# First unit's second-layer weight sums on VectorE, and bias vectors' products held to their units

## Chip, cores and metric

The kernel runs on one core of a Trainium2 chip. The metric is the device time of one launch in microseconds (us), taken as the median over several runs.

## What is computed

The reference applies two layers to a batch of 2 images with 512 channels and 32 x 32 positions. Layer 0 is deformable attention with a learned position bias, then an output projection and an MLP. Layer 1 is plain attention over all 1024 positions. The part that the change touches is the end of layer 0 and the preparation of layer 1:

```python
# layer 0
out = jnp.einsum('bchw,oc->bohw', out, out_w) + out_b[None, :, None, None]     # output projection
x = x + out
xn2 = _bn(x, bn2_g, bn2_b)
h1 = jax.nn.gelu(jnp.einsum('bchw,oc->bohw', xn2, mlp_w1) + mlp_b1[...], approximate=False)
x = x + jnp.einsum('bchw,oc->bohw', h1, mlp_w2) + mlp_b2[...]
# layer 1
q = xt @ Wq.T + bq ; k = xt @ Wk.T + bk ; v = xt @ Wv.T + bv
attn = softmax(q @ k.T / sqrt(c)) ; out = (attn @ v) @ Wp.T + bp ; x = x + out
```

## The kernel before

**Tiling.** Channels lie on the 128 partitions, four blocks of channels per image. A matrix product of 512 x 512 weights with 512 x 1024 activations is done by a fast scheme with seven block products in place of eight (names 1 to 7 in `PARTS`, which gives the left and the right block of each). Each block product is eight multiplications of 128 x 128 by 128 x 512 on TensorE into one PSUM buffer of 128 x 1024. The scheme needs sums of the weights' blocks and differences of the activations' blocks. `fold` (L102) makes the four sums of a weight tile, on the engine that it is given (its instructions carry L105); `spread` (L107) makes the four differences of an activation tile on VectorE (L111 and L114). `plus` (L122) is the eviction of a PSUM buffer by an addition on VectorE (L123). `multiply` (L116) goes through the products in a given order and calls the eviction of each.

**Stages.** Most of the span, to about 1895 us, is the position bias: a long loop of small multiplications (L635). Then come, in order:

- `project(0)` and `project(1)` (L894): the output projection of the two images, with tiles `op0x`, `op0w`, `opt` and `op1x`, `op1w`. The evictions that also add the output bias are L908. PSUM is used through a pool of three buffers here, and a second small pool beside it.
- `normalise(0)` (L938): eight activations on ScalarE that make `xb`, the normalised first image; `spread` makes its differences.
- The MLP in eight units, (image, part) with four parts of 512 hidden channels each. A unit is `layer1` (L959: seven products into `hm`, GELU on ScalarE, `spread` of `hm`) and `layer2` (L992: seven products onto the residual `xs` or an accumulator `acc`). PSUM is used through a new pool of four buffers, `mq`, that takes the place of the earlier two. `normalise(1)` stands in the fourth unit.
- Layer 1 in the same manner (L1079 on).

**Weights of the MLP.** `load_unit` (L877) loads the two weight tiles of a unit, `w1t` and `w2t` (two buffers each, shared with `op1x` and `op1w`), from SP's queue, and makes the sums of both on GpSimd. The first unit's tiles are loaded amid the loads of `xs`; the second unit's when the projection has let go of the buffers; each later unit's when the unit two before it is done with its own.

**Bias vectors' products.** Layer 1's matrix for queries and keys is folded into one, and the value and output matrices into another. What is left of the bias vectors is eight products of a row block `wr` (128 x 512, loaded from `wlt`) with a broadcast row `br` (loaded from `brow`), summed along the row into one column of `ub`. One of them stands in each unit (L1060). `wr` has one buffer, so a load waits for the product before it; `br` changes after the fourth. GpSimd then makes `uc` (L1070) and adds `bp` (L1071). Their readers are in layer 1, from 2342 us on.

**Order.** The program text isn't the order of execution on an engine. A planner takes the traced instructions and orders each engine's queue by when, in its own reckoning, operands and buffers come free. `tc.issue_after(ins)` holds the instructions traced inside it behind `ins`, if they are on the same engine; it makes no wait between engines. `newest(engine)` (L253) gives the instruction traced last for an engine. Before, neither the sums nor the products of L1060 have such an edge.

## Time and profile before

| what | us |
|---|---|
| median of 3 runs (2647.37 to 2648.81) | 2648.25 |
| the profiled execution, its own time | 2648.76 |
| its span, first to last instruction | 2647.0 |
| TensorE busy (99% of the span) | 2628.8 |
| VectorE busy (85%) | 2240.1 |
| ScalarE busy (64%) | 1693.2 |
| GpSimd busy (30%) | 791.0 |

Times in the timeline count from the first instruction of the span. A row of the timeline has the start, the length, the engine, the line, the operation with the tiles that it writes and reads, the size and the number of instructions merged; in brackets stands the idle time of the engine before it, and what ended it. A row of the table by stretches has each engine's busy time with the count of instructions in brackets, and then the granted clock of TensorE.

### The profile page before, as it was taken

The page shows a single profiled execution, that of the slowest core. Times are in us where ns is not written, and L with a number is a line of the kernel's source. Part 1 is how long each engine was busy: PE and PEld are TensorE (multiplying, and loading weights), DVE is VectorE, ACT ScalarE, POOL GpSimd, SP SyncE. Part 2 cuts the span into 40 slices and gives each one's busy share as a digit, 9 for nine tenths or more (in the row PEclk, how much of TensorE's full clock was granted, in tenths as well). Part 3 has the DMA queues.
Part 4 walks back from the last instruction along what each step waited for, and adds up shares of the span by engine and source line. Part 5 has one row for each costly group of instructions (what it writes and reads, how often), then busy time and mean ns, then how long its engine had stood idle before and what let it go on. Part 6 is the DMA issues. An engine that isn't in the chain of part 4 may idle for free.

```text
span 2647.0 us, 46958 instructions
## 1 busy us (share of the span) xinstructions
PE 2628.8 (99%) x19368; PEld 953.9 (36%) x19368; DVE 2240.1 (85%) x1329; ACT 1693.2 (64%) x2222; POOL 791.0 (30%) x867
## 2 busy tenths in 40 slices
PE   9999999999999999999999999999999999999999
PEld 3333322333333233233333323333334444446454
DVE  7999999999999999999999999999674483466354
ACT  5887898888888878887887777777521131114041
POOL 1333333333333333333333333333432232000000
PEclk9999999999999999999999999999999999999999
DMA  5788977888878888887887888788721111000000
GB/s 188 178 178 173 199 166 167 179 182 197 177 169 180 178 178 193 173 177 169 182 183 169 176 177 182 168 174 185 193 96 33 47 48 48 0 17 0 32 1 32
DMA packets 116294, 366.77 MB, mean 139 GB/s; under 512 B 23376, under 2 KB 27616, under 8 KB 113392
## 3 DMA queue, kind: packets, MB, share of 16 engines
q0 software_dynamic: 69408, 235.31, 47.3%
q1 hardware_dynamic: 46240, 128.15, 13.7%
q8 instruction: 153, 2.51, 0.4%
q14 instruction: 61, 0.50, 0.1%
q10 hardware_dynamic: 432, 0.31, 0.0%
HBM read 74.81 MB, written 6.55 MB: 31 GB/s over the span
## 4 chain that ended last, share of the span: by engine, by line
PE 92%; DVE 3%; issue 2%; ACT 2%; DMA 1%; DVEq 0%; POOL 0%; SPq 0%; ACTq 0%; POOLq 0%
PE ps L635 62%; PE sw L953 15%; PE sw L1084 9%; PE sw L1182 2%; PE sim L721 1%; PE psg L537 1%; DVE h L618 1%; PE sw L900 1%; DVE ub L654 0%; DMA wr<-in_wlt 0%; PE pkv L471 0%; DVE xs L908 0%; PE sim L704 0%; PE pt L738 0%; DMA uc<-uo 0%
## 5 line engine op out<-in xcount | busy, mean ns | idle before, releaser
L635 PE MATMUL ps<-h,cw 128*32 128x512 f32 x16384 | 1776.4, 592 | 5.2 <-ACT rx L644 4.0
L618 DVE CUSTOM_DVE_ANT_1 h<-ta,tb 128x4096 f32<-128x4096 f32 (+1 forms) x257 | 1131.2, 4402 | 28.6 <-PE ps L635 25.8
L635 PEld LDWEIGHTS ps<-h,cw 128*32 128x32 f32 x16384 | 543.0, 110 | 1203.1 <-issue 1131.4
L644 ACT ACTIVATE rx<-ps,sc 128x1024 f32<-128x1024 f32 x512 | 567.9, 1109 | 145.1 <-PE ps L635 127.1
L646 ACT ACTIVATE ub<-ps,sc 128x1024 f32<-128x1024 f32 x256 | 308.2, 1204 | 93.6 <-PE ps L635 93.5
L654 DVE SCALAR_TENSOR_TENSOR ub<-rx,sc,ub 128x1024 f32<-128x1024 f32 x256 | 327.1, 1278 | 6.6 <-ACT ub L646 6.6
L673 POOL DMA_DIRECT2D ua<-uc x126 | 158.8, 1275 | 298.6 <-DMA ua<-uc 288.7
L673 POOL DMA_DIRECT2D ua<-ua x189 | 225.9, 1372 | 16.8 <-DMA ua<-uo 11.9
L953 PE MATMUL sw<-xb,w1t 128*128 128x512 f32 x448 | 195.2, 596 | 3.1 <-DVE xs L123 3.1
L656 POOL DMA_DIRECT2D uo<-ub x127 | 125.6, 989 | 233.0 <-DVE ub L654 217.8
L953 PE MATMUL sw<-hm,w2t 128*128 128x512 f32 x448 | 193.6, 592 | 0.0
L646 ACT ACTIVATE uo<-ps,sc 128x1024 f32<-128x1024 f32 x128 | 154.2, 1204 | 53.0 <-PE ps L635 52.7
L654 DVE SCALAR_TENSOR_TENSOR uo<-rx,sc,uo 128x1024 f32<-128x1024 f32 x128 | 163.7, 1279 | 9.0 <-ACT uo L646 9.0
L123 DVE TENSOR_TENSOR hm<-hm,sw 128x1024 f32<-128x1024 f32 x56 | 67.5, 1218 | 105.5 <-PE sw L953 105.3
L673 POOL DMA_DIRECT2D uc<-uo x63 | 53.6, 852 | 313.5 <-DMA uc<-uo 307.4
L953 PEld LDWEIGHTS sw<-xb,w1t 128*128 128x128 f32 x448 | 85.7, 192 | 111.5 <-issue 105.7
L962 ACT ACTIVATE hm<-hm,vs 128x512 f32<-128x512 f32 x64 | 42.5, 713 | 129.0 <-DVE hm L123 129.0
L953 PEld LDWEIGHTS sw<-hm,w2t 128*128 128x128 f32 x448 | 85.1, 190 | 107.1 <-issue 106.4
L123 DVE TENSOR_TENSOR xs<-xs,sw 128x1024 f32<-128x1024 f32 (+1 forms) x48 | 55.6, 1171 | 73.7 <-PE sw L1084 36.0
L656 POOL DMA_DIRECT2D ua<-ub x64 | 58.6, 915 | 179.1 <-DVE ub L654 171.8
L1084 PE MATMUL sw<-aT,vt 128*128 128x512 f32 x224 | 96.7, 593 | 0.3 <-ACT aT L1164 0.3
L987 ACT COPY hm<-sw 128x1024 f32<-128x1024 f32 x8 | 8.1, 1010 | 136.3 <-PE sw L953 136.3
(247 smaller groups left out, 2268.2 us busy)
## 6 DMA issues: line engine op xcount, KB each, us to landing
uo<-ub POOLq DMA_DIRECT2D x127, 512.0 KB, 5.5
fb<-fdr SPq DMA_DIRECT2D x64, 512.0 KB, 5.1
ua<-ub POOLq DMA_DIRECT2D x64, 512.0 KB, 5.5
uc<-ub POOLq DMA_DIRECT2D x64, 512.0 KB, 5.1
ua<-ua POOLq DMA_DIRECT2D x63, 256.0 KB, 6.2
ua<-uo SPq DMA_DIRECT2D x63, 256.0 KB, 2.6
ua<-uo POOLq DMA_DIRECT2D x63, 256.0 KB, 5.7
uc<-uc POOLq DMA_DIRECT2D x63, 256.0 KB, 6.7
```

Source lines behind the costliest of these rows:

```text
L123: nc.vector.tensor_tensor(out, a, b_, op)
L618: nc.vector._custom_dve(TENSOR_ADD_SAT, out=h1[:, y : y + step].rearrange("p y t x -> p (y t x)"), in0=a.unsqueeze(1).to_broadcast([P, ste ...
L635: nc.tensor.matmul(ps[32 * q : 32 * q + 32, h, :], cw2[:, 32 * z : 32 * z + 32], h1[:, 16 * h : 16 * h + 16, q, :], start=True, stop=True,)
L644: nc.scalar.activation(o, ps, AF.Relu, bias=sc[:, 4 + z : 5 + z])
L646: nc.scalar.activation(o, ps, AF.Relu, bias=sc[:, 4 + z : 5 + z], scale=sc[:, z : z + 1])
L654: nc.vector.scalar_tensor_tensor(r[1], r[0], sc[:, z : z + 1], r[1], ALU.mult, ALU.add)
L656: nc.gpsimd.dma_start(out=sums[s][1], in_=sums[s][3], accum_op=ALU.add)
L673: nc.gpsimd.dma_start(out=out, in_=in_, accum_op=ALU.add)
L953: nc.tensor.matmul(ps[:, m, :], w[:, a, k, m * P : (m + 1) * P], x[:, b_, k, :], start=(k == 0), stop=(k == 1),)
L962: nc.scalar.activation(hm[:, blk, m, :], src[:, m, :], AF.Gelu, bias=col("mb1", 4 * p + 2 * (blk // 2) + m), scale=scale,)
L1084: nc.tensor.matmul(ps[:, m, :], w[:, a, k, c + m * P : c + (m + 1) * P], x[b_][:, k, :], start=(k == 0), stop=(k == nk - 1),)
L1182: nc.tensor.matmul(v[:, m, :], xbl[b_][:, k, m * P : (m + 1) * P], gn[:, a, k, :], start=(k == 0), stop=(k == 1),)
```

## The change

Two things are changed. The four sums of the first unit's `w2t` are no longer made by GpSimd in `load_unit`; VectorE makes them, traced after `project(1)` and held behind the instruction that was traced last for VectorE, which is the last eviction of `project(1)`. And each of the eight products of L1060 is held behind the instruction traced last for VectorE at that point, which is the last difference of `hm` in its own unit's `layer1`. The helper `newest` is moved up so that both places can use it.

```diff
@@ -50,6 +50,9 @@
+    def newest(engine):
+        return next(i for i in reversed(nc.cur_bb.bb.instructions) if i.engine == engine)
@@ -249,9 +252,6 @@
-        def newest(engine):
-            return next(i for i in reversed(nc.cur_bb.bb.instructions) if i.engine == engine)
@@ -879,7 +879,8 @@
             for i, w in enumerate((w1, w2)):
                 wt = wp.tile([P, 7, 2, 256], F32, name=f"w{i + 1}t")
                 nc.sync.dma_start(out=wt[:, 0:4], in_=w[:, p])
-                fold(nc.gpsimd, [wt[:, j] for j in range(7)])
+                if (b, p, i) != (0, 0, 1):
+                    fold(nc.gpsimd, [wt[:, j] for j in range(7)])
                 ws_.append(wt)
@@ -1035,6 +1036,8 @@
         xb = normalise(0)
         spread(op1[1])
         project(1, *op1, op1w[:, 3:5].rearrange("p a k n -> p a (k n)"))
+        with tc.issue_after(newest(mybir.EngineType.DVE)):
+            fold(nc.vector, [wts[units[0]][1][:, j] for j in range(7)])
         spread([xb[:, j] for j in range(7)])
         load_unit(*units[1])
@@ -1057,9 +1060,11 @@
             layer1(p, wa, xb, hm)
-            nc.vector.scalar_tensor_tensor(
-                wr, wr, 1.0, br, ALU.mult, ALU.mult, accum_out=ub[:, j, k : k + 1]
-            )
+
+            with tc.issue_after(newest(mybir.EngineType.DVE)):
+                nc.vector.scalar_tensor_tensor(
+                    wr, wr, 1.0, br, ALU.mult, ALU.mult, accum_out=ub[:, j, k : k + 1]
+                )
             if p == NU - 1 and b == 0:
                 xb = normalise(1)
```

## Prediction

> **What bounds the kernel now.** I read the page first, then the busy time by stretches around the change, then the timeline of each engine there, and last the chain of waits. The page says that TensorE is busy for nearly the whole span:

> ```profile
> PE 2628.8 (99%) x19368; PEld 953.9 (36%) x19368; DVE 2240.1 (85%) x1329; ACT 1693.2 (64%) x2222; POOL 791.0 (30%) x867
> ```

> So only 18 us are not TensorE's. The table by stretches shows where part of them lie: one stretch has 21.29 of 26.90 us busy, and the next runs at a granted clock of 0.94.

> ```profile
> core 0: us, PE busy (x) PEld busy (x) DVE busy (x) ACT busy (x) POOL busy (x), PEclk, DMA share, GB/s
> 1911.50:1925.50 14.00, 14.00 (x36) 6.10 (x34) 13.96 (x11) 1.01 (x1) 12.64 (x7) 1.00 0.44 164
> 1925.50:1952.40 26.90, 21.29 (x50) 9.04 (x49) 24.11 (x32) 6.65 (x9) 0.64 (x1) 0.99 0.23 79
> 1952.40:1978.00 25.60, 25.60 (x56) 11.31 (x57) 11.44 (x12) 6.30 (x8) 15.86 (x13) 0.94 0.34 123
> ```

> The stretch is the output projection of the second image, project(1). TensorE's timeline names the releaser of each gap; all are VectorE's evictions of PSUM buffers:

> ```profile
> 1922.01 3.60 PE L900 MATMUL sw<-qa,vp 128*128 128x512 f32 x8
> 1927.28 3.70 PE L900 MATMUL sw<-qa,vp 128*128 128x512 f32 x8 [1.67 <-DVE xs L123]
> 1935.22 3.67 PE L900 MATMUL sw<-op1x,op1w 128*128 128x512 f32 x8 [0.81 <-DVE xs L908]
> 1952.32 25.85 PE L953 MATMUL sw<-xb,w1t 128*128 128x512 f32 x56 [3.12 <-DVE xs L123]
> 1978.00 24.20 PE L953 MATMUL sw<-hm,w2t 128*128 128x512 f32 x56
> ```

> VectorE's timeline shows what keeps it late. Between the evictions stand bias vectors' products (L1060), two of which wait for their row to arrive; and two operations take 2.28 us that take 1.22 elsewhere:

> ```profile
> 1914.67 2.28 DVE L114 SCALAR_TENSOR_TENSOR op1x<-op1x,qa 128x1024 f32<-128x1024 f32 x1
> 1916.88 2.28 DVE L111 TENSOR_TENSOR qa<-qa 128x1024 f32<-128x1024 f32 x1
> ...
> 1930.59 0.69 DVE L1060 SCALAR_TENSOR_TENSOR wr<-wr,br 128x512 f32<-128x512 f32 x1 [1.63 <-DMA wr<-in_wlt]
> ...
> 1950.43 0.69 DVE L1060 SCALAR_TENSOR_TENSOR wr<-wr,br 128x512 f32<-128x512 f32 x1 [0.77 <-DMA wr<-in_wlt]
> ...
> 1951.05 1.22 DVE L123 TENSOR_TENSOR xs<-xs,sw 128x1024 f32<-128x1024 f32 x1
> 1961.11 1.22 DVE L123 TENSOR_TENSOR hm<-hm,sw 128x1024 f32<-128x1024 f32 x1 [8.85 <-PE sw L953]
> ```

> GpSimd's sums lie beside the slow ones:

> ```profile
> 1909.90 5.97 POOL L105 TENSOR_TENSOR w1t<-w1t 128x512 f32<-128x512 f32 x4 [6.33 <-DMA w1t<-in_w]
> 1915.83 8.38 POOL L105 TENSOR_TENSOR w2t<-w2t 128x512 f32<-128x512 f32 x4
> ```

> The chain of waits agrees: from 1911 to 1952 it runs through VectorE and the loads of wr; after 1952.32 it is TensorE's multiplications alone.

> [...] 2.28 against 1.22 us beside the sums, while evictions, which read PSUM, keep 1.21 us at 1919.08. [...] Here a gap of 3.12 us sufficed: weight loads from 1952.3 to 1955.0 stand about 0.85 us apart instead of 0.43; after the gaps of 1.67 and 0.81 us none do.

> **The accounting.** A product is eight multiplications; seven take 24.03 us where nothing waits (2026.07 to 2050.10), so 3.433 each. From project(1)'s first product (1922.01) to the second unit's start (2002.04) are 80.03 us for 21 products, which need 72.10. The excess is 7.93: 1.84 and 0.98 at the two gaps, 0.18 at two restarts, 3.29 before layer1 of the first unit, and 1.65 in that layer1 (25.68 for 24.03), the slow restart. This is all that the change can win here.

> **The change part by part.**

> *GpSimd gives up four sums (8.38 us).* VectorE's L114 at 1914.67 is still blocked until the w1 sums end (1915.83), so it ends at 1916.95 as now. From there nothing blocks it: the difference qa ends at 1918.1, the eviction into opt at 1919.2, the next difference at 1920.35, the four L908 (2.73 for four uncontended, from 1945.80) at 1923.0 instead of 1926.1. That wins 3.1 us on VectorE. The two last evictions of project(0) end at 1924.15 and 1925.3; the first frees the buffer for the second product, which TensorE reaches at 1925.44. The gap of 1.67 goes.

> *Bias products leave project(1).* Five stand there, 0.70 us each with the accumulator read (3.5), and 2.4 us of waits on wr. What is late next is ScalarE: its eight normalising activations (5.75 us) wait for L908's last reading of opt, so they run 1923.1 to 1928.85; the difference L114 of xb needs the last, ends at 1930.2, and the two L908 behind it free product one's buffer at 1931.5. TensorE needs it at 1932.3: 0.8 us to spare, and the gap of 0.81 goes. With VectorE's order otherwise as now, its later evictions follow TensorE. The last product ends at 1946.04 (1922.01 + 7 x 3.433). Its eviction begins 0.20 later (as at 2012.54 for a product ended at 2012.34), takes 1.22, and TensorE starts 0.05 after that: 1.47 us, short enough not to halve the clock.

> *Four sums on VectorE.* One of this size takes 0.686 us there (op0w at 1431.4), 1.26 on GpSimd; four are 2.74. The edge puts them behind the last eviction, where VectorE now idles 8.85 us. Contended with GpSimd's sums for the second unit, which start about then, three of 1.26 us go between: 6.5 us, still inside. They are needed only in layer2, 24 us later. I take nothing; without that cover they would cost 2.74 to 6.5.

> *Bias products in their units.* Each now waits behind layer1's last difference; behind it on VectorE queue layer2's evictions. Price 0.70 free; beside a GpSimd sum up to 1.9 (1.21 blocked, 0.69 work). Four PSUM buffers give about 3 us of slack in most units. The tight place is the change of images, where VectorE has no idle time from 2125.18 to 2171.9: the eviction at 2160.25 frees its buffer at 2161.46, needed at 2163.40. Slack 1.9 against 0.7 to 1.9: cost 0 to 0.5, I take 0.2. A gain is excluded, as TensorE has no gap there.

> *SP.* The loads of wr, issued early one after another now, each wait for the preceding unit's product, some 48 us apart. In SP's order the second may stand before the weights of a later unit. Even before the second unit's, it would release them near 1986; landing takes 4.9 us (w2t), sums about 8 with contention, against a first need at about 2000.7: 0 to 2.8 us. I take 0, since the traced order loads those weights first. The second row br waits for the fourth product and has a unit's time. *GpSimd's* small addition uc, which now waits 21.74 us in its queue, must wait for the fourth unit's product (about 2136); even if sums stood behind it they are used after 2146. Its reader is at 2349. Zero. Moving newest() up costs nothing.

> Sum: 7.93 - 1.47 = 6.46, less 0.2 for the change of images and 0.1 for a restart like that at 1927.28: **6.2 us**, the whole of which reaches the end, since TensorE is dense after. The profiled execution took 2648.76 (span 2647.0 and 1.76 around it), 0.51 above the median of 2648.25. Its span would become 2640.8, its time 2642.56, the median 2642.0.

> **Rivals.**

> *A, ScalarE's chain keeps half.* If the activations start no earlier than now (1926.18), because their memory is released by something else or the blocking by GpSimd isn't what is thought, product one's buffer comes free at 1935.08 as now. Product 6 starts at 1935.22 and TensorE ends at 1949.03; only the bias product before the last eviction is won: TensorE restarts at 1950.5, 1.8 us earlier, without the slow restart (1.65). Gain 3.5: 2644.8. For it: the margin is only 0.8 us. Against it: L908 is named as releaser, and its slow part lies wholly beside GpSimd's sums.

> *B, the sums push back the differences of xb; slower.* They are traced before those differences. If the planner keeps that order, layer1's second product, which needs a difference, waits. Sums from 1947.46, contended: 6.5 us; two differences, each behind a sum of 1.26: 4.8 more, so 1958.8 against a need at 1950.94: 7.8 us and a slow restart of 1.65, together 9.5 against 6.46 won. 2651.3; if all four differences must be done (8 x 1.26 + 4 x 0.68 + 4 x 1.13), 2657.3. It decides against the change from a wait of 4.8 us on. Against it: now the differences stand at 1931 to 1940, inside project(1), drawn by their inputs' arrival, which the change doesn't alter.

> *C, it doesn't do what it says:* an edge holds only operations of one engine, and the sums' place can only be later, so I give this none of its own.

> **How the numbers follow.** A measurement of this kernel can tell about 0.2% (5.3 us) from no change: 2643.0 and 2653.5 are the borders. Forecast 0.70, all faster, its own range 2641.0 to 2643.0 (slack at the change of images used up; repeats spread by 1.4). A 0.16, within. B 0.14: 0.05 within, 0.09 slower. Faster 0.70, same 0.21, slower 0.09. The range of 8 in 10 takes in the forecast and most of A: 2640.5 to 2647.0.

> **What would show it.** After, TensorE should start layer1 some 25.5 us after project(1)'s first product (now 30.3), with an idle of about 1.3 us, no clock below 0.99 in the 26 us behind it, and no gap inside project(1). L111 at 1916.88 should take 1.22, L908's four end near 1923. The sums should stand between the last xs eviction and the first hm eviction. I am wrong if differences of xb stand behind the sums, if TensorE idles near the change of images by more than 1 us, or if the activations on xb start near 1926.

## The result, and the profile after

The median of 17 runs is 2643.17 us (2641.37 to 2647.41), beside 2649.43 us (2646.7 to 2651.31) for 17 runs of the kernel before on the same chips. The ratio is 0.9978, with a 95% interval from 0.9972 to 0.9984: 5.8 us less, 4.2 to 7.4. The forecast was 6.2 us less. The median itself lies 0.2 us above the narrow range of the forecast (2641.0 to 2643.0) and within the wide one; in these runs the kernel before was itself 1.2 us slower than the 2648.25 that the forecast started from.

Lines have moved. In the kernel after, evictions by `plus` are L126 (L123 before), the differences of `spread` L114 and L117 (L111 and L114 before), the sums of `fold` L108 (L105), the evictions with the output bias L909 (L908), the MLP's multiplications L954 (L953), the bias vectors' products L1065 (L1060). The kernels of the experiments differ from this by a few lines.

The table by stretches of the kernel after, cut 3.5 us behind the start of project(1) as before, and at the first unit's layer1, answers to the two poor rows of before:

```profile
core 0: us, PE busy (x) PEld busy (x) DVE busy (x) ACT busy (x) POOL busy (x), PEclk, DMA share, GB/s
1929.40:1951.40 22.00, 20.68 (x50) 8.86 (x48) 18.34 (x20) 4.38 (x6) 0.00 (x0) 1.00 0.11 38
1951.40:1975.50 24.10, 24.10 (x56) 10.74 (x57) 10.74 (x10) 6.29 (x8) 15.31 (x12) 1.00 0.26 97
```

Of 5.6 us without TensorE in that part, 1.3 are left, and the granted clock in the first unit's layer1 is 1.00 where it was 0.94. TensorE's timeline has one wait in place of three:

```profile
1925.89 7.03 PE L901 MATMUL sw<-qa,vp 128*128 128x512 f32 x16
1932.75 7.03 PE L901 MATMUL sw<-op1x,op1w 128*128 128x512 f32 x16
...
1946.49 3.60 PE L901 MATMUL sw<-op1x,vp 128*128 128x512 f32 x8
1951.40 24.30 PE L954 MATMUL sw<-xb,w1t 128*128 128x512 f32 x56 [1.31 <-DVE xs L126]
1975.54 24.20 PE L954 MATMUL sw<-hm,w2t 128*128 128x512 f32 x56
1999.57 5.74 PE L954 MATMUL sw<-xb,w1t 128*128 128x512 f32 x13
```

The second unit began here before:

```profile
2002.04 24.20 PE L953 MATMUL sw<-xb,w1t 128*128 128x512 f32 x56
```

From project(1)'s first product (1925.89) to the second unit (1999.57) are 73.68 us, 80.03 before (1922.01 to 2002.04): 6.35 less. This stretch is read below for all kernels that touch it, from one profiled execution of each. From the second unit to the end of the span are 645.2 us, 644.9 before, so the rest of the kernel takes what it took, but for 0.27.

The profiled execution's span fell by 2.2 only, to 2644.8, because project(1) began 3.88 us later in it (1925.89 against 1922.01). In the ten profiled kernels of this study, whose long loop is the same code, the start of project(1) lies anywhere between 1921.62 and 1927.39. In the long loop of this execution TensorE waited 6.0 us for ScalarE's `rx` and 1.5 for loads; before it was 4.0 and 0.3. The medians average this out; a single span doesn't.

VectorE's timeline shows the steps:

```profile
1918.71 2.29 DVE L117 SCALAR_TENSOR_TENSOR op1x<-op1x,qa 128x1024 f32<-128x1024 f32 x1
1920.92 1.21 DVE L114 TENSOR_TENSOR qa<-qa 128x1024 f32<-128x1024 f32 x1
...
1924.32 2.73 DVE L909 SCALAR_TENSOR_TENSOR xs<-xs,vs,opt 128x512 f32<-128x512 f32 x4
...
1934.06 1.40 DVE L909 SCALAR_TENSOR_TENSOR xs<-xs,vs,sw 128x512 f32<-128x512 f32 x2
...
1950.12 1.22 DVE L126 TENSOR_TENSOR xs<-xs,sw 128x1024 f32<-128x1024 f32 x1 [1.19 <-PE sw L901]
1951.26 3.68 DVE L108 TENSOR_TENSOR w2t<-w2t 128x512 f32<-128x512 f32 x4
1958.64 1.22 DVE L126 TENSOR_TENSOR hm<-hm,sw 128x1024 f32<-128x1024 f32 x1 [3.69 <-PE sw L954]
```

The difference of `qa` takes 1.21 us (2.28 before), the four evictions behind it 2.73, for 4.75 before:

```profile
1921.35 4.75 DVE L908 SCALAR_TENSOR_TENSOR xs<-xs,vs,opt 128x512 f32<-128x512 f32 x4
```

The last eviction of project(1) is no longer late: VectorE waits for TensorE's last product (1.19 us), and the 1.31 us of waiting that are left to TensorE cover that eviction (1.22). The four sums stand behind it and end 3.69 us before VectorE has other work. No bias product stands in this part; the first is at 1986.18.

### The profile page after: what moved, and what is told of

Read it like the earlier page. It is cut to its first block, busy times and chain, and to the rows that moved or that the text cites. A ratio compares the mean times of both kernels' runs of the same rounds, so it can differ in the third digit from the quotient of the medians.

```text
span 2644.8 us, 46954 instructions
## 1 busy us (share of the span) xinstructions
PE 2627.7 (99%) x19368; PEld 956.5 (36%) x19368; DVE 2244.6 (85%) x1333; ACT 1693.5 (64%) x2222; POOL 783.9 (30%) x863
## 4 chain that ended last, share of the span: by engine, by line
PE 84%; DVE 7%; issue 5%; DMA 2%; ACT 2%; POOL 0%; DVEq 0%; SPq 0%; POOLq 0%; ACTq 0%
PE ps L635 53%; PE sw L954 15%; PE sw L1089 9%; DVE h L618 3%; PE sw L901 2%; PE sw L1187 2%; DVE ub L654 1%; PE sim L721 1%; PE psg L537 1%; DMA uc<-uo 1%; DVE uo L654 1%; DVE acc L334 0%; DMA ua<-uc 0%; DVE ua L654 0%; DVE uc L654 0%
## 5 line engine op out<-in xcount | busy, mean ns | idle before, releaser
L954 PE MATMUL sw<-xb,w1t 128*128 128x512 f32 x448 | 193.7, 592 | 1.3 <-DVE xs L126 1.3
L954 PE MATMUL sw<-hm,w2t 128*128 128x512 f32 x448 | 193.6, 592 | 0.0
L126 DVE TENSOR_TENSOR hm<-hm,sw 128x1024 f32<-128x1024 f32 x56 | 67.5, 1218 | 107.2 <-PE sw L954 107.0
L954 PEld LDWEIGHTS sw<-xb,w1t 128*128 128x128 f32 x448 | 85.0, 190 | 108.8 <-issue 105.0
L954 PEld LDWEIGHTS sw<-hm,w2t 128*128 128x128 f32 x448 | 85.0, 190 | 107.5 <-issue 106.5
L126 DVE TENSOR_TENSOR xs<-xs,sw 128x1024 f32<-128x1024 f32 (+1 forms) x48 | 55.6, 1171 | 72.0 <-PE sw L1089 36.0
L598 ACT ACTIVATE ta<-fb,vs 128x512 f32<-128x512 f32 (+1 forms) x65 | 89.0, 1371 | 10.9 <-DMA fb<-fdr 10.9
```

What stands on the lines that cost most here:

```text
L126: nc.vector.tensor_tensor(out, a, b_, op)
L598: nc.scalar.activation(ta.rearrange("p j x -> p x j")[:, :, j0:j1], fb[:, 0, :, j0:j1], AF.Identity, bias=col("cb1"), scale=col("w1x"),)
L954: nc.tensor.matmul(ps[:, m, :], w[:, a, k, m * P : (m + 1) * P], x[:, b_, k, :], start=(k == 0), stop=(k == 1),)
```

## Experiments

**The two halves, each alone.** First the sums without the holds (the code of this section is shown in part):

```diff
-            with tc.issue_after(newest(mybir.EngineType.DVE)):
-                nc.vector.scalar_tensor_tensor(wr, wr, 1.0, br, ...)
+            nc.vector.scalar_tensor_tensor(wr, wr, 1.0, br, ...)
```

> The sums of the first unit's w2t on VectorE as in the change, the bias products free as before. I go by the stretch from the first product of project(1) to the first product of the second unit, which took 80.03 us before and 73.68 after and has 72.10 of multiplications; the whole time scatters by some 2 us from the long loop before it. Theory (the sums on GpSimd blocked VectorE for 3.1 us; the bias products and their waits on wr are a second cause): the gap of 1.67 us goes, VectorE still ends late behind the fifth product, TensorE restarts about 3.1 us earlier than before: stretch 75.3, or 77.0 if the idle time before the first unit is still near 3 us and the restart is slow. Rival (the bias products alone matter): stretch near 80. Rival (the sums alone matter): near 73.7.

The stretch is 77.20 us (1923.31 to 2000.51): 2.83 won, and the second of the two values expected. The ratio of times is 0.9993 (0.9985 to 1.0001), which can't tell 2.8 us from nothing. TensorE's timeline of this kernel has no marked gap in project(1), and 0.19 us of delay in the row of 7.22 us (7.03 with the change). But the wait before the first unit stays long, and its layer1 takes 25.84 us for 24.03:

```profile
1930.17 7.22 PE L901 MATMUL sw<-op1x,op1w 128*128 128x512 f32 x16
...
1950.64 26.00 PE L954 MATMUL sw<-xb,w1t 128*128 128x512 f32 x56 [2.95 <-DVE xs L126]
1976.48 24.20 PE L954 MATMUL sw<-hm,w2t 128*128 128x512 f32 x56
```

What holds VectorE there is seen in its own timeline, a bias product that waits for its row ahead of the last eviction. The wait and the product, 1.2 us, are most of the 1.64 by which this gap is longer than with the change:

```profile
1948.76 0.69 DVE L1064 SCALAR_TENSOR_TENSOR wr<-wr,br 128x512 f32<-128x512 f32 x1 [0.58 <-DMA wr<-in_wlt]
1949.37 0.08 DVE L1064 DVE_READ_ACCUMULATOR wr<-wr,br 128x1 f32 x1
1949.37 1.22 DVE L126 TENSOR_TENSOR xs<-xs,sw 128x1024 f32<-128x1024 f32 x1
```

Then the holds without the sums:

```diff
-                if (b, p, i) != (0, 0, 1):
-                    fold(nc.gpsimd, [wt[:, j] for j in range(7)])
+                fold(nc.gpsimd, [wt[:, j] for j in range(7)])
...
-        with tc.issue_after(newest(mybir.EngineType.DVE)):
-            fold(nc.vector, [wts[units[0]][1][:, j] for j in range(7)])
```

> The bias products held to their units as in the change, the sums of the first unit's w2t on GpSimd as before. Theory: VectorE is still blocked by GpSimd's sums, so the gap of 1.67 us at the second product of project(1) stays, a gap of about 0.3 us at product 6 follows; behind the last product nothing is late, idle time before the first unit 1.3 us and no slow restart: stretch (80.03 before, 73.68 after) 75.9. Rival (the sums alone matter): near 80. Rival (the bias products alone matter): near 73.7.

The stretch is 76.56 us (1923.75 to 2000.31): 3.47 won, with a ratio of 0.9993 (0.9985 to 1.0002). It is 0.66 longer than expected. 0.46 of this is the early gap, 2.13 us for 1.67 before: GpSimd's sums ended 2.67 us after project(1)'s first product here, and 2.20 before. TensorE's timeline is the mirror image of the last, an early gap and a short late one; the gap at product 6 is 0.24 us, for 0.81 before:

```profile
1929.48 3.70 PE L900 MATMUL sw<-qa,vp 128*128 128x512 f32 x8 [2.13 <-DVE xs L126]
...
1952.14 24.30 PE L953 MATMUL sw<-xb,w1t 128*128 128x512 f32 x56 [1.31 <-DVE xs L126]
```

VectorE's timeline shows why. With GpSimd's sums of `w2t` running from 1918.03 to 1926.42 beside them, the difference of `qa` takes 2.28 us again, and the four evictions 4.75:

```profile
1923.55 4.75 DVE L908 SCALAR_TENSOR_TENSOR xs<-xs,vs,opt 128x512 f32<-128x512 f32 x4
```

So both halves are needed, and they add: 2.83 + 3.47 = 6.30 against 6.35 together. The sums remove the early gap, the holds shorten the late one and with it the slow restart. The rivals in which one half does it all are out. Whether the bias products held VectorE more by their own 0.7 us or by the waits for their rows wasn't separated.

**The place of the sums.** The change without the edge that puts the sums behind project(1):

```diff
-        with tc.issue_after(newest(mybir.EngineType.DVE)):
-            fold(nc.vector, [wts[units[0]][1][:, j] for j in range(7)])
+        fold(nc.vector, [wts[units[0]][1][:, j] for j in range(7)])
```

> The change without the edge that puts the four sums behind project(1). The planner then draws them between the last evictions of project(0) and the first difference of xb. Theory: VectorE waits there for ScalarE (0.78 and 1.60 us in the changed kernel), which covers most of 2.74 us; product one's buffer comes free about 0.3 us later and 0.4 us before TensorE needs it: stretch 73.7 to 74.0, the edge wins nothing by itself. Rival (the cover behind the projection is what makes the sums free): a gap of 1 to 2.7 us in project(1), stretch 75 to 76.5.

The stretch is 73.68 us (1927.39 to 2001.07), as with the edge; the ratio is 0.9983 (0.9974 to 0.9991). VectorE's timeline shows the sums where it waits for ScalarE with the change (0.78 and 1.60 us, before the first two differences of `xb`):

```profile
1929.48 0.68 DVE L108 TENSOR_TENSOR w2t<-w2t 128x512 f32<-128x512 f32 x1
1930.09 1.21 DVE L126 TENSOR_TENSOR xs<-xs,sw 128x1024 f32<-128x1024 f32 x1
1931.22 1.89 DVE L108 TENSOR_TENSOR w2t<-w2t 128x512 f32<-128x512 f32 x3
```

The edge on the sums wins nothing by itself; taking them off GpSimd does. There are two covers, and either is enough.

**Rival B made on purpose.** The differences of `xb` are held behind the sums:

```diff
-        spread([xb[:, j] for j in range(7)])
+        with tc.issue_after(newest(mybir.EngineType.DVE)):
+            spread([xb[:, j] for j in range(7)])
```

> The change, and the four differences of xb held behind the four sums: the order of the prediction's rival B, made on purpose. Theory: the sums take 3.7 us as in the changed kernel, then each difference stands behind a GpSimd sum of 1.26 us; the one that the second product of layer1 needs is done some 8.3 us after TensorE restarts, 4.9 us late, and TensorE restarts at half clock (1.65): stretch 80.2, as before the change, up to 83 if more of GpSimd's sums go between. Rival (the differences have slack even there): stretch 73.7.

The stretch is 81.53 us (1922.34 to 2003.87), 7.85 more than with the change, and the kernel is no faster than before, by its time 0.1% slower: 1.0009 (1.0003 to 1.0016). TensorE waits for the difference that layer1's second product needs, and then restarts slowly: from 1957.02 to 1979.83 are 22.81 us for six products that need 20.60.

```profile
1947.85 3.70 PE L954 MATMUL sw<-xb,w1t 128*128 128x512 f32 x8 [1.31 <-DVE xs L126]
1957.02 22.98 PE L954 MATMUL sw<-xb,w1t 128*128 128x512 f32 x48 [5.47 <-DVE xb L117]
1979.83 24.20 PE L954 MATMUL sw<-hm,w2t 128*128 128x512 f32 x56
```

On VectorE, the sums and both differences are stretched by GpSimd's sums for the second unit (1948.79 to 1955.79 and on):

```profile
1947.71 4.75 DVE L108 TENSOR_TENSOR w2t<-w2t 128x512 f32<-128x512 f32 x4
1952.39 2.28 DVE L114 TENSOR_TENSOR xb<-xb 128x1024 f32<-128x1024 f32 x1
1954.70 2.17 DVE L117 SCALAR_TENSOR_TENSOR xb<-xb 128x1024 f32<-128x1024 f32 x1
```

The rival was a real one. In the change the planner drew these differences into project(1), at 1930 to 1941, and that kept it from happening.

**The change of images.** In the kernel after, the fifth unit takes 48.32 us on TensorE (2143.77 to 2192.09), 0.25 over its multiplications. First, three more products like the fourth unit's, behind it:

```diff
+                if i == NU - 1:
+                    for _ in range(3):
+                        nc.vector.scalar_tensor_tensor(wr, wr, 1.0, br, ALU.mult, ALU.mult, accum_out=uc[:, 0:1])
```

> The change, with three more multiplications of the same kind and size on VectorE behind the fourth unit's bias product (their sums go into a column that is written over later). This asks for the slack at the change of images. There the fifth unit took 48.32 us on TensorE after the change, of which 48.07 are multiplications. Theory (the slack of 1.9 us is used up by the one product of 1.75): three more of 0.70 go straight to TensorE, the fifth unit takes 48.3 + 2.1 = 50.4, and 0.9 less or more by the planner's new order there. Rival (the 0.26 us have another cause, the slack is still there): 48.3 to 48.5.

The fifth unit takes 49.54 us (2144.10 to 2193.64), 1.22 more, where 2.1 were expected, 0.9 less or more by the planner's order. (This kernel was timed once only, 2648.08 us, with a long wait of its own in the long loop; only its timeline is used.) TensorE's timeline names the releaser, and it isn't a PSUM buffer:

```profile
2144.10 24.20 PE L954 MATMUL sw<-xb,w1t 128*128 128x512 f32 x56
2169.53 24.27 PE L954 MATMUL sw<-hm,w2t 128*128 128x512 f32 x56 [1.23 <-ACT hm L963]
2193.64 24.20 PE L954 MATMUL sw<-xb,w1t 128*128 128x512 f32 x56
```

layer2 waits for ScalarE's GELU of `hm`, which waits for VectorE's evictions. The block of five evictions that feeds it began 19.68 us after the fifth unit's start before the change, 20.78 after it, and 21.99 here. From 1.10 late come 0.19 us of delay on TensorE (2167.99 for 2167.80), from 2.31 late come 1.40: the slack was 0.9 us in both. VectorE itself is later than with the change by 1.21 of the 2.1 us that were added. The planner's order is a new one there, and some operations have other durations (three additions to `xs` take 5.63 us, 6.70 with the change); which of the two took up the rest wasn't separated.

Then the fourth unit's product held behind the third unit's last eviction, where VectorE idles:

```diff
+            if i == NU - 1:
+                bias()          # the product with its edge, ahead of layer1
             layer1(p, wa, xb, hm)
...
+            if i != NU - 1:
+                bias()
```

> The change, but the fourth unit's bias product is held behind the last eviction of the third unit, so that it falls into VectorE's idle time of 5.7 us at the start of the fourth unit's layer1, not into the full stretch at the change of images. Theory: the fifth unit takes 48.07 us on TensorE in place of 48.32 and nothing else moves; 0.25 us is below what the times can tell. Rival (the 0.26 us don't come from the bias product): 48.32.

```profile
2143.26 24.20 PE L954 MATMUL sw<-xb,w1t 128*128 128x512 f32 x56
2167.30 24.20 PE L954 MATMUL sw<-hm,w2t 128*128 128x512 f32 x56
2191.33 24.20 PE L954 MATMUL sw<-xb,w1t 128*128 128x512 f32 x56
```

The fifth unit takes 48.07 us in TensorE's timeline of this kernel: the 0.25 us are the fourth product's. The ratio, 0.9979 (0.9972 to 0.9985), can't be told from that of the change, 0.9978.

**The other sums too.** Those of the first unit's `w1t` also go to VectorE:

```diff
-                if (b, p, i) != (0, 0, 1):
+                if (b, p) != (0, 0):
                     fold(nc.gpsimd, [wt[:, j] for j in range(7)])
...
-            fold(nc.vector, [wts[units[0]][1][:, j] for j in range(7)])
+            for w in wts[units[0]]:
+                fold(nc.vector, [w[:, j] for j in range(7)])
```

> The change, and the sums of the first unit's w1t too go from GpSimd to VectorE, behind project(1) beside those of w2t. Theory (VectorE is no longer late in project(1)[...]): its operations beside the sums of w1t shrink from 2.6 and 2.3 us to 1.4 and 1.2, product one's buffer comes free about 2 us earlier, and the stretch from project(1) to the second unit stays at 73.7; the eight sums take 5.5 to 8 us, and the one that layer1's second product needs is done in time. Rival [...]: stretch 72.5. Rival (the sums of w1t come too late there): 75 or more.

The stretch stays at 73.68 us (1921.62 to 1995.30); 0.9979 (0.9972 to 0.9986). VectorE's timeline has the short durations (1.22 us where the change has 2.29 at 1918.71). Two sizes came out otherwise than expected. The eight sums take 10.3 us (1947.00 to 1957.25) for 5.5 to 8 expected, with GpSimd's sums for the second unit beside them from 1948.28 on, and product one's buffer is free only 1.0 us earlier, not 2:

```profile
1913.23 1.22 DVE L117 SCALAR_TENSOR_TENSOR op1x<-op1x,qa 128x1024 f32<-128x1024 f32 x1
...
1948.20 4.03 DVE L108 TENSOR_TENSOR w1t<-w1t 128x512 f32<-128x512 f32 x3
1952.15 5.10 DVE L108 TENSOR_TENSOR w2t<-w2t 128x512 f32<-128x512 f32 x3
```

The operations that are still long with the change (2.29 us for 1.22) cost nothing by now: VectorE waits for TensorE in project(1), 1.19 us before the last eviction. Both edits together:

> The two edits before this one together, as the version with the least idle time that these readings suggest. Theory: stretch 73.7, fifth unit 48.07, time the same as that of the change within what can be told. Rival: the sums of w1t on VectorE cost or win something, seen as in the run with both sums.

Stretch 73.68 us (1923.19 to 1996.87), fifth unit 48.07, ratio 0.9981 (0.9974 to 0.9988). None of the last three versions is told from the change by its time. What is left in this part is the 1.31 us in which TensorE waits for the last eviction as the PSUM pools change over; taking that away wasn't tried.

## Why the prediction was right

Point by point, with the prediction's times put beside the first product of project(1), which stood at 1922.01:

- *GpSimd's sums block VectorE for 3.1 us.* The four evictions were to end 1.0 us after project(1)'s first product; they end 1.16 after, 4.09 before. The first gap is gone, and with the sums back on GpSimd it is 2.13 us: shown. GpSimd's timeline of before shows how the long operations lie beside the sums: two sums end at 1915.87 and 1918.07, and VectorE's two operations of 2.28 us end 1.1 us behind them, at 1916.95 and 1919.16. With the sums of `w1t` also on VectorE the same two take 1.22 (1913.23 and 1914.37). By what the two engines hold each other up, no trace shows.

```profile
1914.16 1.71 POOL L105 TENSOR_TENSOR w1t<-w1t 128x512 f32<-128x512 f32 x1
1915.83 2.24 POOL L105 TENSOR_TENSOR w2t<-w2t 128x512 f32<-128x512 f32 x1
```

- *ScalarE's chain is next and has 0.8 us to spare.* Its activations on `xb` were to start 1.1 us after the first product; they start 1.24 after (1927.13). Product one's buffer is free at 1935.46, TensorE needs it at 1936.19: 0.73 to spare. Rival A, in which these activations start no earlier (4.17 us after it, as before), is out:

```profile
1927.13 5.75 ACT L944 ACTIVATE xb<-xs,vs,bns 128x512 f32<-128x512 f32 x8 [10.33 <-DVE xs L909]
```

- *The last product, its eviction, the restart.* 25.5 us from project(1)'s first product to layer1 were expected, with about 1.3 idle; measured 25.51 and 1.31. There is no slow restart: layer1 takes 24.14 us, the 0.1 over 24.03 that was taken.
- *The sums on VectorE cost nothing.* 3.68 us, between the 2.74 and 6.5 named, and covered.
- *SP and GpSimd cost nothing.* SP issues the second unit's weights at 1947.94 and 1950.11, ahead of the second `wr` at 1987.97. `uc` is made at 2133.33, after 0.64 us of waiting in place of 21.74.
- *The change of images costs 0.2 us.* 0.25 measured, but the step behind it failed: I reckoned with the release of a PSUM buffer and a slack of 1.9 us. The wait is for ScalarE's GELU of `hm`, with a slack of 0.9 us. The product itself took 1.75 us there, within the 0.7 to 1.9 named, but VectorE came only 1.10 late: a subtraction (L866) that GpSimd's sums had stretched to 2.28 us before took 1.21, and one of the additions to `acc` took 1.79 for 1.22. By the prediction's own terms, 1.75 against a slack of 1.9, nothing would have reached TensorE. The 0.2 is right by luck.
- *The sum.* 6.35 in the stretch less 0.25 is 6.1 us; predicted were 6.46 less 0.1 and 0.2. The medians differ by 6.26, and the interval of the ratio, 4.2 to 7.4, holds both. The 80.03 us of before are one execution, and the sums' place beside project(1) moves a little from run to run (0.5 us between the two kernels that have them on GpSimd), so the agreement to a tenth is in part chance.
- *Rival B's price.* 9.5 us were predicted, 7.85 came: the wait for the difference was 5.47 (7.8 was taken, but fewer of GpSimd's sums went between: VectorE's four took 4.75 us, not 6.5), the slow restart 2.21 (1.65).

## What to carry to other kernels

Where a dense engine has a gap, count its products from a point before the gap to one behind it and compare with the time that they need: the excess is all that there is to win. It can be read to a tenth of a microsecond in one execution where the kernel's time scatters by several, and it shows halves of a change that the time can't tell. Work that is free of hurry (here the bias products and half of the sums) should be kept from an engine that hands buffers back, and also from one beside whose work that engine's operations take longer (GpSimd here, beside whose sums VectorE's differences take 2.28 us for 1.21). Where it goes then matters less than that it is gone, as long as nothing that is needed next is put behind it.

## What was not expected of the hardware

```profile
1948.65:1952.06 3.41, 0.54 (x2) 0.00 (x0) 2.64 (x4) 0.00 (x0) 0.00 (x0) 1.00 0.77 264
1952.06:1955.47 3.41, 3.15 (x4) 1.51 (x5) 0.20 (x1) 0.00 (x0) 0.00 (x0) 0.50 1.00 393
```

With the sums alone, the clock falls 0.30 us after TensorE has restarted (1950.64), for one window:

```profile
1947.53:1950.94 3.41, 0.46 (x2) 0.30 (x2) 2.83 (x5) 0.00 (x0) 0.00 (x0) 1.00 0.84 277
1950.94:1954.36 3.42, 3.42 (x5) 1.33 (x4) 2.15 (x4) 0.00 (x0) 0.91 (x1) 0.50 0.98 390
```

The kernel with three more products has a window in its long loop with 2.52 us without TensorE, and pays as well:

```profile
250.35:253.76 3.41, 0.89 (x12) 0.16 (x8) 3.41 (x3) 3.07 (x4) 0.76 (x2) 1.00 0.11 38
253.76:257.17 3.41, 3.41 (x20) 0.87 (x16) 2.69 (x2) 2.56 (x5) 2.75 (x4) 0.50 1.03 240
```

With the holds alone, the gap of 2.13 us doesn't; the next product loses only 0.1 (3.70 us for 3.60), as after 1.31 and 1.67 us:

```profile
1927.70:1931.11 3.41, 1.63 (x4) 0.87 (x5) 2.86 (x3) 2.73 (x4) 0.00 (x0) 1.00 0.00 0
1931.11:1934.53 3.42, 3.42 (x9) 1.52 (x8) 1.59 (x2) 3.42 (x6) 0.00 (x0) 1.00 0.00 0
```

TensorE was busy for 16, 13, 26 and 48% of the first window of these pairs. In the traces of before and after, the clock fell behind the windows in which TensorE was busy 16% (the one above), 19% and 37% (both at the end of the span), and behind none with 45% or more. The nearest to these is in the kernel after, with 1.52 us busy and the clock at 1.00 behind it:

```profile
249.39:252.80 3.41, 1.52 (x16) 0.26 (x8) 3.41 (x4) 2.87 (x4) 1.50 (x3) 1.00 0.19 59
252.80:256.22 3.42, 3.41 (x32) 1.07 (x36) 3.42 (x2) 3.39 (x5) 2.01 (x3) 1.00 0.99 219
```

The loss is about half of the time that TensorE works at a granted clock of 0.50, and the 0.1 of a restart: 3.15 us of such work before lose 1.65 in all, 3.42 with the sums alone 1.81. With the differences behind, the loss was 2.21. That the share in such a window decides, and not the length of the gap, is my reading of these rows and isn't shown: no run moved a gap against the windows to test it.

The price doesn't follow the length alone: the gap of 3.12 us before cost 1.65 in the restart, the shorter one of 2.95 with the sums alone cost 1.81. A wait that is cut from 3.1 to 1.3 us was worth 3.4 here, not 1.8.
